# Stores of a batch's odd blocks moved from SyncE's queue to ScalarE's in a recommender kernel

## The chip, the cores and the metric

The kernel runs on one core of one Trainium2 chip. The metric is the device time of the whole program in microseconds (us). Most executions agree within 0.3%.

## The reference, cut to what matters

A table of 100001 items (rows of 128 floats) is gathered for 1024 users and 50 steps, averaged, normalized and run through a spiking neuron; the mean spike count of each user is then multiplied with the whole table.

```python
e = emb[seq]                                   # 1024 x 50 x 128
uF = jnp.cumsum(e, axis=1) / denom[:, :, None]
y = (uF - mean) * lax.rsqrt(var + BN_EPS) * gamma + beta
_, spikes = lax.scan(step, v0, x_seq)          # 50 steps
uF_out = spikes.mean(axis=0)                   # 1024 x 128
scores = uF_out @ emb.T                        # 1024 x 100001, 409.6 MB
```

## The kernel before

The first stage computes the spike counts, one step after another. The second stage goes through the table in 25 chunks of 4096 items (the last is shorter). A chunk is loaded seven chunks ahead (2 MB), transposed on TensorE into PSUM and split into a rounded part by ScalarE (`hi`) and the remainder by VectorE (`lo`). For each of the eight blocks `n` of 128 users it makes a tile of 128 x 4096 scores in four pieces `q` of 1024 columns: TensorE multiplies into a PSUM tile, VectorE evicts (copies from PSUM into the output buffer) pieces 0 and 2, ScalarE pieces 1 and 3, and the tile is stored (2 MB). (The first block of the first chunk is done apart.)

```python
def store(n, c0, o):
    nc.sync.dma_start(out=out[n * P : (n + 1) * P, c0 : c0 + o.shape[1]], in_=o)
...
op = ctx.enter_context(tc.tile_pool(name="o", bufs=3, reuse_waits="tile"))
psum = ctx.enter_context(
    tc.tile_pool(name="psum", bufs=4, space=bass.MemoryType.PSUM, reuse_waits="tile")
)
...
for c, (c0, w) in enumerate(chunks):
    for n in range(NB):
        o = op.tile([P, CH], F32, tag="o", name=f"o_{c}_{n}")
        for q in range(-(-w // HALF)):
            po = psum.tile([P, HALF], F32, tag="ps", name=f"po_{c}_{n}_{q}")
            for k0 in range(0, hw, BANK):
                product(po[:, k0 : k0 + BANK], c, q, n, k0, min(BANK, hw - k0))
            if turn % 2 == 0:
                nc.vector.tensor_scalar_mul(o[:, h0 : h0 + hw], po[:, :hw], 1.0 / T)
            else:
                nc.scalar.mul(o[:, h0 : h0 + hw], po[:, :hw], 1.0 / T)
            turn += 1
            if n == NB - 1 and q < 2:
                ready(c + 1, 2 + q)      # a quarter of the next chunk: transpose, hi, lo
        store(n, c0, o[:, :w])           # cut: the first chunk's exceptions
        if n in (2, 5):
            ready(c + 1, n // 5)
    if c + AHEAD < len(chunks):
        fetch(c + AHEAD, rowp)           # the load, by nc.sync
```

Two pools: three output buffers `o` in SBUF, and four PSUM slots.

Of the kernel before, what the change touches and what calls it, by code (L numbers as in the profile page):

```python
# [20 lines left out]
P = 128  # L21
# [10 lines left out]
def rec_kernel(  # L32
# [9 lines left out]
    nc = tc.nc  # L42
# [109 lines left out]
            )  # L152

    def store(n, c0, o):
        nc.sync.dma_start(out=out[n * P : (n + 1) * P, c0 : c0 + o.shape[1]], in_=o)


    with ExitStack() as ph:
# [193 lines left out]
        o = gp.tile([P, HALF], F32, tag="e", name="o_0_0_0")  # L352
        for h, po in enumerate(pre):
            product(po, 0, 0, 0, h * BANK, BANK)
        step(halves[1])
        nc.scalar.mul(o[:, :BANK], pre[0], 1.0 / T)
        store(0, 0, o[:, :BANK])
        lower(0, 3, pt)
        nc.vector.tensor_scalar_mul(o[:, BANK:], pre[1], 1.0 / T)
        store(0, BANK, o[:, BANK:])  # L360
        spiked(countB, slice(P, BANK), vt)
        spiked(countC, halves[1], vt)
        for q in range(1, 4):
            o = (up if q == 3 else gp).tile([P, HALF], F32, tag="uF" if q == 3 else "e", name=f"o_0_0_{q}")
            po = (accp if q % 2 == 0 else vp).tile(
                [P, HALF], F32, tag="v0" if q % 2 else "pt", name=f"po_0_0_{q}"
            )
            for k0 in range(0, HALF, BANK):
                product(po[:, k0 : k0 + BANK], 0, q, 0, k0, BANK)
            for h, cs in enumerate(halves):  # L370
                if h == 0:
                    nc.scalar.mul(o[:, cs], po[:, cs], 1.0 / T)
                else:
                    nc.vector.tensor_scalar_mul(o[:, cs], po[:, cs], 1.0 / T)
            store(0, q * HALF, o)
# [13 lines left out]
    for c, (c0, w) in enumerate(chunks):  # L389
        for n in range(NB):  # L390
            if c == 0 and n == 0:
                continue
            o = op.tile([P, CH], F32, tag="o", name=f"o_{c}_{n}")
# [40 lines left out]
```

## Time and profile before

| | before |
|---|---|
| time, median of the first 3 runs | 1699.22 us |
| first store issued | 597.00 us |
| DMA share of the second stage, 597 to 1699 us | 0.99, at 405 GB/s |
| one store, one load (2.1 MB each) | about 5 us and 6.4 us of all DMA engines (estimates of the prediction) |
| issue of a store by SyncE | 0.33 us |
| output buffers, PSUM slots | 3, 4 |

The DMA share is the mean busy share of the core's 16 DMA engines: at 0.99 the data movers set the pace, and every other engine's idle time is slack. The lines are shown in the prediction.

### The profile page before, as it was taken

What the parts mean: (1) busy time and instruction counts of PE and PEld (TensorE: products, weight loads), DVE (VectorE), ACT (ScalarE), POOL (GpSimd) and SP (SyncE); (2) the same over time, 40 slices, a digit from 0 to 9 for tenths busy, and PEclk for the clock granted to TensorE, in tenths of its full rate; (3) what the DMA queues carried; (4) which work ended last, traced back from release to release, by engine and by line L of the source; (5) the groups of instructions that cost most, each with busy time, mean ns of one, the idle gap of its engine ahead of it and who ended that gap; (6) DMA issues with size and microseconds to landing.
All of it is one profiled execution on the core that took longest, in us unless ns stands there. A gap on an engine that the chain in (4) does not pass through costs nothing.

```text
span 1698.7 us, 12572 instructions
## 1 busy us (share of the span) xinstructions
PE 1055.1 (62%) x4434; PEld 808.9 (48%) x4434; DVE 1000.2 (59%) x1211; ACT 631.3 (37%) x697; POOL 379.1 (22%) x406
## 2 busy tenths in 40 slices
PE   3222323232223297887777787777777778888886
PEld 2111212122122276665566665666655556766664
DVE  5577778776768874554455454554454555555553
ACT  2122222222222354444444444444444444444442
POOL 7666666666666200000000000000000000000000
PEclk9999999999998598999999999899999899999998
DMA  9211111111111089999999999999999999999998
GB/s 342 100 45 47 46 46 48 49 46 45 47 45 47 22 351 408 424 424 409 410 402 412 401 400 399 411 413 407 407 403 407 398 404 395 424 418 418 414 414 348
DMA packets 58412, 488.15 MB, mean 287 GB/s; under 512 B 12491, under 2 KB 13292, under 8 KB 33772
## 3 DMA queue, kind: packets, MB, share of 16 engines
q1 hardware_dynamic: 45548, 461.10, 66.2%
q0 software_dynamic: 12800, 26.24, 5.3%
q8 instruction: 35, 0.57, 0.1%
q14 instruction: 29, 0.24, 0.0%
HBM read 77.69 MB, written 409.60 MB: 287 GB/s over the span
## 4 chain that ended last, share of the span: by engine, by line
DMA 42%; DVE 24%; PE 16%; another core or an unknown queue 7%; ACT 7%; issue 3%; SPq 0%; POOL 0%; ACTq 0%; DVEq 0%; POOLq 0%
DMA scores<-o 41%; PE po L146 15%; ACT o L403 5%; DVE bs L292 4%; DVE uF L291 4%; DVE v L323 4%; DVE count L261 3%; DVE s L306 3%; DVE negv L328 2%; DVE o L401 2%; ACT v L320 1%; DVE a L314 1%; DMA e<-in_L_rec_emb_table,idx 1%; DVE mv L296 1%
## 5 line engine op out<-in xcount | busy, mean ns | idle before, releaser
L401 DVE TENSOR_SCALAR o<-po 128x1024 f32<-128x1024 f32 x390 | 462.9, 1220 | 472.6 <-DMA scores<-o 355.7
L403 ACT ACTIVATE o<-po 128x1024 f32<-128x1024 f32 (+1 forms) x390 | 385.8, 1018 | 573.6 <-DMA scores<-o 359.6
L146 PE MATMUL po<-hi,countC 128*128 128x512 f32 x784 | 344.1, 439 | 154.0 <-ACT o L403 153.8
L185 POOL DMA_INDIRECT e<-in_L_rec_emb_table,idx x400 | 378.5, 946 | 188.6 <-issue 107.9
L146 PE MATMUL po<-lo,countC 128*128 128x512 f32 x784 | 329.5, 421 | 0.0
L250 PE MATMUL pre<-zT,l 128*128 128x512 f32 x100 | 77.6, 778 | 383.6 <-DVE uF L291 329.8
L146 PEld LDWEIGHTS po<-hi,countC 128*128 128x128 f32 x784 | 163.5, 209 | 214.6 <-ACT o L403 181.2
L146 PE MATMUL po<-hi,countB 128*128 128x512 f32 x588 | 234.5, 399 | 22.3 <-ACT o L403 21.8
L250 PEld LDWEIGHTS pre<-zT,l 128*128 128x128 f32 x100 | 28.8, 289 | 425.5 <-issue 310.7
L146 PE MATMUL po<-lo,countB 128*128 128x512 f32 x588 | 229.5, 391 | 0.0
L146 PEld LDWEIGHTS po<-lo,countC 128*128 128x128 f32 x784 | 162.8, 208 | 32.2
L300 ACT ACTIVATE r<-mv,eps 128x1 f32<-128x1 f32 x50 | 14.7, 294 | 392.2 <-DVE mv L296 230.2
L134 DVE TENSOR_TENSOR lo<-pt,hi 128x1024 fp32r<-128x1024 f32 x98 | 117.3, 1216 | 47.9 <-ACT hi L130 47.9
L291 DVE SCALAR_TENSOR_TENSOR uF<-rlen,pre 128x512 f32<-128x512 f32 x100 | 67.8, 678 | 128.0 <-remote 112.1
L146 PEld LDWEIGHTS po<-hi,countB 128*128 128x128 f32 x588 | 110.7, 188 | 54.9 <-ACT o L403 31.8
L101 PE MATMUL pt<-ident,rows 128*128 128x128 f32 x782 | 107.2, 281 | 44.7 <-ACT o L403 38.3
L101 PEld LDWEIGHTS pt<-ident,rows 128*128 128x128 f32 x782 | 91.0, 144 | 70.3 <-ACT o L403 55.8
L146 PEld LDWEIGHTS po<-lo,countB 128*128 128x128 f32 x588 | 110.8, 188 | 21.9
L130 ACT CAST hi<-pt 128x1024 fp32r<-128x1024 f32 x98 | 99.0, 1010 | 42.1 <-PE pt L101 41.7
L282 PE MATMUL pre<-ident,e 128*128 128x128 f32 x400 | 98.5, 418 | 10.4 <-DMA e<-in_L_rec_emb_table,idx 8.7
L282 PEld LDWEIGHTS pre<-ident,e 128*128 128x128 f32 x400 | 83.2, 220 | 24.1 <-DMA e<-in_L_rec_emb_table,idx 12.3
L146 PE MATMUL po<-hi,countA 128*128 128x512 f32 x194 | 76.9, 396 | 1.1 <-ACT o L403 1.1
(61 smaller groups left out, 680.4 us busy)
## 6 DMA issues: line engine op xcount, KB each, us to landing
scores<-o SPq DMA_DIRECT2D x190, 2048.0 KB
rows<-in_L_rec_emb_table SPq DMA_DIRECT2D x24, 2048.0 KB
scores<-o SPq DMA_DIRECT2D x8, 848.5 KB
e<-in_L_rec_emb_table,idx POOLq DMA_INDIRECT x400
scores<-o SPq DMA_DIRECT2D x2, 1024.0 KB
scores<-o SPq DMA_DIRECT2D x3, 512.0 KB
scores<-o SPq DMA_DIRECT2D x2, 256.0 KB
rows<-in_L_rec_emb_table SPq DMA_DIRECT2D x1, 512.0 KB
```

Source lines behind the costliest of these rows:

```text
L101: nc.tensor.transpose(pt[:, k0 : k0 + kw], rows[c][:kw, q * KQ + k0 // P, :], ident[:kw, :kw])
L130: nc.scalar.copy(vh, vp)
L134: nc.vector.tensor_tensor(vl, vp, vh.bitcast(F32), ALU.subtract)
L146: nc.tensor.matmul(po[:, :kw], lhsT=counts[n], rhs=part[:, k0 : k0 + kw], start=j == 0, stop=j == 1,)
L185: nc.gpsimd.indirect_dma_start(out=es[t][:, n * P : (n + 1) * P], out_offset=None, in_=table, in_offset=bass.IndirectOffsetOnAxis(ap=idx[: ...
L250: nc.tensor.matmul(pre[h], lhsT=l, rhs=zT[:, h * BANK : (h + 1) * BANK], start=t == 0, stop=False, skip_group_check=True,)
L282: nc.tensor.matmul(pre[h][:, k : k + P], lhsT=e[:, h * BANK + k : h * BANK + k + P], rhs=ident, start=False, stop=last, is_transpose=True, ...
L291: nc.vector.scalar_tensor_tensor(uF[:, cs], rlen[:, cs], 1.0 / (t + 1), pre[h], ALU.max, ALU.mult)
L292: nc.vector.bn_stats(bs[:, h, :], uF[:, cs])
L323: nc.vector.scalar_tensor_tensor(vt[:, cs], negv[:, cs], -0.5, vt[:, cs], ALU.mult, ALU.add)
L401: nc.vector.tensor_scalar_mul(o[:, h0 : h0 + hw], po[:, :hw], 1.0 / T)
L403: nc.scalar.mul(o[:, h0 : h0 + hw], po[:, :hw], 1.0 / T)
```

## The change

The intent: two hardware queues for the stores, so that the issuing work is shared and two stores can be under way at once. Blocks with an even `n` stay with SyncE, as do all loads.

```diff
     def store(n, c0, o):
-        nc.sync.dma_start(out=out[n * P : (n + 1) * P, c0 : c0 + o.shape[1]], in_=o)
+
+        engine = nc.scalar if n % 2 else nc.sync
+        engine.dma_start(out=out[n * P : (n + 1) * P, c0 : c0 + o.shape[1]], in_=o)
```

## The prediction

> **What bounds the kernel now.** I read the page first (slices, DMA queues, chain), then the waits by engine, then the windows of the second stage, then the timeline at the end of a chunk of the table. The page's 40 slices show two stages: a first of 14 slices (about 597 us) in which VectorE leads and the DMA engines do little, and a second of 26 slices with the DMA row at 8 to 9.
>
> ```profile
> DVE  5577778776768874554455454554454555555553
> DMA  9211111111111089999999999999999999999998
> GB/s 342 100 45 47 46 46 48 49 46 45 47 45 47 22 351 408 424 424 409 410 402 412 401 400 399 411 413 407 407 403 407 398 404 395 424 418 418 414 414 348
> q1 hardware_dynamic: 45548, 461.10, 66.2%
> HBM read 77.69 MB, written 409.60 MB: 287 GB/s over the span
> DMA scores<-o 41%; PE po L146 15%; ACT o L403 5%; DVE bs L292 4%; DVE uF L291 4%; DVE v L323 4%; DVE count L261 3%; DVE s L306 3%; DVE negv L328 2%; DVE o L401 2%; ACT v L320 1%; DVE a L314 1%; DMA e<-in_L_rec_emb_table,idx 1%; DVE mv L296
> ```
>
> The stores to scores are 41% of the chain, and one hardware queue carries all 461 MB. The change touches only stores, and the first one is issued at 597.00, so the first 597 us are not in play.
>
> The windows view of the second stage and of the ends of chunks (columns: busy time and count of PE, PEld, DVE, ACT, POOL; granted clock; DMA share; GB/s):
>
> ```profile
> 597.00:1699.00 1102.00, 877.22 (x3883) 688.52 (x3881) 575.17 (x492) 479.47 (x487) 0.00 (x0) 0.93 0.99 405
> ...
> 1418.00:1423.00 5.00, 3.77 (x21) 2.96 (x21) 3.26 (x3) 2.80 (x4) 0.00 (x0) 1.00 1.03 436
> 1423.40:1425.00 1.60, 1.60 (x8) 1.31 (x7) 1.17 (x2) 0.77 (x2) 0.00 (x0) 1.00 0.15 61
> 1507.00:1508.40 1.40, 1.40 (x8) 1.17 (x7) 0.96 (x2) 0.57 (x2) 0.00 (x0) 1.00 0.37 152
> ```
>
> Over 1102 us the mean DMA engine is busy 0.99 of the time: the stage is bound by the data movers. Only for about 1.5 us at the end of a chunk does the share fall (0.15 and 0.37 here), and no wait of an issuing sequencer on a transfer explains that. The waits:
>
> ```profile
> SPq L155 <- DVE o L401: 966.8, 198, 11.6
> ACT o L403 <- DMA scores<-o: 359.6, 128, 9.1
> DVE o L401 <- DMA scores<-o: 355.7, 129, 7.9
> ```
>
> SyncE's queue waits for the evictions (the data to be stored), hardly for anything else, and the evictions wait for an output buffer to be emptied by a store. That circle says: three output buffers, emptied at the pace of the DMA engines. The issue itself is small:
>
> ```profile
> 1003.03 0.33 SPq L155 DMA_DIRECT2D scores<-o  x1
> 1003.46 0.39 SPq L79 DMA_DIRECT2D rows<-in_L_rec_emb_table  x1
> ```
>
> 0.33 us per store against about 5 us that a 2 MB store occupies the engines: SyncE issues for some 205 x 0.33 = 68 us of the 1102.
>
> **What the Trainium skill says.** "DMA: Bandwidth & Descriptors", section "Issuing engines are not separate DMA queues": DMAs from SyncE and ScalarE run on the same 16 engines and interleave, and issuing from several engines saves only the sequencer's issue time. The trace agrees with its premise: 0.33 us of issue beside 5 us of transfer. Same page, "Specifications": the fabric's ceiling is 435 GB/s; the trace has 436 in its best 5 us window and 405 over the stage, so little room is left. Same page, "Queues, rings and completion order": each DMA engine takes turns, packet by packet, between the queues that have work; with one queue for all stores, no view of before shows it for two stores. The page "Perfetto Trace Analysis", section "Identifying Performance Opportunities", says that a gap repeating on the engine that should be saturated can mean too few buffers; the dip at each chunk's end looks like one.
>
> **The change part by part.** The order view of both programs: SyncE goes from 237 to 137 instructions, ScalarE from 698 to 799; every computing instruction stays in its place, the waits of the evictions are for the same stores, and the table loads stay with SyncE. So 100 issues move.
>
> (1) SyncE loses 100 x 0.33 = 33 us of issue. It was idle for 967 us waiting for VectorE, so this is worth 0.
>
> (2) ScalarE gains 100 issues, about 100 x 0.33 = 33 us if they cost it the same, plus a wait for VectorE in front of each. In a tile of four halves VectorE evicts two (2 x 1.22, merged 2.35 us) and ScalarE two (1.94 us), started together, so ScalarE waits about 0.4 us: 100 x 0.4 = 40 us. ScalarE was busy 479 of 1102 us; with 73 more it has 550 us idle. Most of that idle time is the wait for a buffer, which lies just after the issue, so the cost on the path is near 0; only in front of the casts of the next chunk's table and of an eviction whose buffer is already free can up to 0.7 us show. One such place per chunk at its end, 24 x 0.7 = 17 us off the path, of which I count 2.
>
> (3) The bytes are the same: 409.6 MB out and, in this stage, 405 GB/s x 1102 us - 409.6 = 37 MB in. No byte is saved.
>
> (4) The loads. Load issue to load issue is 46.96 us (1003.46 to 1050.42); the chunks late in the kernel, without a load, take 40.5 us (dip at 1507.0 to dip at 1547.7). So a 2.1 MB load occupies 6.4 us, 328 GB/s, where the stores run at 16.8 MB / 40.5 = 414. If alternating with ScalarE's stores hid all of that slowness, 17 loads x (6.4 - 5.06) = 23 us would be won. I count a quarter: -5.
>
> (5) The release of buffers. With one queue a store gets all engines and buffers come free one at a time, every 5 us; when one comes free, two untouched stores (10 us of work) are still ahead of the engines. With two queues two stores share: when one ends, its companion may be almost done, and 5 to 10 us of work are left. The refill takes 2.4 us of eviction and about 1 us of issue and start (an estimate from the two timelines) where TensorE had run ahead, and 4.7 us at a chunk's end (eviction starts at 1419.72, store issued at about 1424.4), where the casts and subtractions of the next chunk lie between. So only at the chunk's end can the engines run dry longer, by perhaps 0.5 us, 24 times: 12 us; and once per load, when SyncE's stores stand behind the load while ScalarE's queue empties, by up to 1 us, 17 times. I count a third of the 29: +10, less the 3 that staggering might give back: +7.
>
> Sum: 0 + 2 + 0 - 5 + 7 = +4 us on 1699: 1703, and as I do not trust the signs of (4) and (5), I pull it towards no change: 1701.
>
> **The rivals.** Rival A: interleaving makes the transfers better, hiding the slowness of loads and the dips. For: 6.4 us for a load, dips to 0.15. At the very most it wins the 23 us of (4) and the dips, (1 - 0.15) x 1.6 = 1.4 and (1 - 0.37) x 1.4 = 0.9, about 1 us x 24 = 24: 47 us, 1652. Against: the dips come when a chunk's last tile is not evicted yet, and a second queue evicts nothing. Rival B: buffers come free in pairs, and evictions, TensorE and transfers fall into step: bursts with the engines dry in between. For: only three buffers, and slack at chunk ends is already used up. With 2 us per chunk and 2 per load: 24 x 2 + 17 x 2 = 82 us, 1780. Against: in mid-chunk the refill of 3.4 us fits into the 5 us that are left at worst. Rival C: ScalarE's in-order stream becomes the bound, as its issue waits for VectorE. Against: 550 us of idle time; it would take over 5 us per store. Rival D, which I believe: work is conserved, the engines stay at 0.99, and nothing happens beyond a few us.
>
> **Range and chances.** D with the terms above gives 1685 to 1715; part of A would go to 1680, part of B to 1725. Range 1682 to 1724. Faster by over 2% needs under 1665, nearly all of A: 4%. Slower by over 2% needs over 1733, half of B: 8%. Within 2%: 88%.
>
> **What would show it.** Right: two hardware queues with about 200 MB of stores each, ScalarE's queue (L157) with 100 or so issues near 0.33 us, DMA share still 0.98 or more from 597 us on, issue-to-issue of the loads within 0.7 us of 46.9. Step (4) right: chunks with a load shorter while those without stay at 40.5. Step (5) right: the dips at chunk ends longer, or new ones after each load, and the evictions' waits for stores in fewer and longer pieces. Wrong: if DMA share falls below 0.97, buffers are the bound and B holds; if GB/s at the same share rises above 415, A holds; if ScalarE's evictions wait less for stores and VectorE's more, C holds.

## More of the kernel before

The runs came from different chips: on some of them the kernel before took about 1616 us, on others 1694 to 1700, because the first stage ends earlier there (first store at 513 us in the profile of run e4, at 597 in that of the kernel before). The stage that matters here is as long on both. Every experiment is therefore compared with runs of the kernel before on its own chip.

## The result, and the profile after

The changed kernel took 1747.9 us (median of 4 runs, 1745.9 to 1750.7) against 1699.4 us: a ratio of 1.0286, 95% interval 1.0268 to 1.0304. Ratios are the mean time of one kernel's fast runs over that of the other's of the same rounds, so not quite the ratio of the medians. The change lost 48.5 us and was outside the predicted range. The granted clock is not the reason: in the four runs the mean was 0.78, 0.92, 0.78 and 0.93, and the times do not follow it. Its low values come from the first stage.

The page of the changed kernel, its DMA rows and its two store queues:

```profile
DMA  9211111111111299999999999999999999989998
GB/s 343 91 46 46 44 47 45 49 49 44 45 48 46 93 384 398 393 389 404 385 397 395 375 392 383 397 387 381 395 392 394 373 393 375 420 363 405 421 422 340
q1 hardware_dynamic: 31004, 256.29, 37.2%
q10 hardware_dynamic: 14544, 204.81, 27.8%
```

The windows view over the second stage of the changed kernel, and over a stretch within one chunk (columns as in the prediction; the last two are DMA share and GB/s):

```profile
597.00:1744.00 1147.00, 919.62 (x3883) 710.37 (x3882) 582.23 (x493) 486.89 (x488) 0.00 (x0) 0.92 0.96 390
...
1056.00:1061.00 5.00, 3.27 (x14) 2.07 (x13) 2.45 (x2) 1.64 (x2) 0.00 (x0) 1.00 0.76 321
1061.00:1064.00 3.00, 3.00 (x19) 2.58 (x18) 0.00 (x0) 2.04 (x2) 0.00 (x0) 1.00 0.66 268
```

The same 461.10 MB pass (256.29 + 204.81) in a stage that is 45 us longer. The DMA share fell from 0.99 to 0.96, which is 0.03 x 1147 = 34 us of idle data movers, and the dips are no longer only at the ends of chunks. (Most of the rest is in the packets: the packed traces hold the time of each, which no view prints. Summed over these queues and divided by 16 engines it grew from 1125.2 to 1134.7 us.)

Who keeps them waiting? The view of waits, before and after (columns: total us, times, longest):

```profile
ACT o L403 <- DMA scores<-o: 359.6, 128, 9.1
...
ACT o L403 <- PE po L146: 213.0, 145, 3.1
```

```profile
ACT o L405 <- PE po L146: 434.4, 302, 5.8
...
DVE o L403 <- DMA scores<-o: 211.0, 52, 6.6
...
ACT o L405 <- DMA scores<-o: 180.3, 45, 7.0
...
PE po L146 <- DVE o L403: 142.7, 115, 3.9
```

Before, the evictions mostly waited for a store to free a buffer. After, ScalarE's evictions wait twice as long for TensorE (434 instead of 213 us), and half as long for stores (180 instead of 360). The buffers had become free, but the products were not there. Yet TensorE has no more work than before. The timeline of one odd tile (block 5) in the changed kernel shows why:

```profile
1056.50 1.23 DVE L403 TENSOR_SCALAR o<-po 128x1024 f32<-128x1024 f32 x1 [0.61 <-PE po L146]
...
1057.40 1.03 ACT L405 ACTIVATE o<-po 128x1024 f32<-128x1024 f32 x1 [0.79 <-PE po L146]
1057.78 0.50 PE L146 MATMUL po<-hi,countC 128*128 128x512 f32 x1 [0.41 <-DVE o L403]
...
1059.03 1.22 DVE L403 TENSOR_SCALAR o<-po 128x1024 f32<-128x1024 f32 x1 [1.30 <-PE po L146]
1060.31 0.50 PE L146 MATMUL po<-hi,countC 128*128 128x512 f32 x1 [1.32 <-DVE o L403]
...
1061.53 1.02 ACT L405 ACTIVATE o<-po 128x1024 f32<-128x1024 f32 x1 [3.11 <-PE po L146]
...
1062.59 0.34 ACTq L157 DMA_DIRECT2D scores<-o  x1
```

Read it as a chain: the eviction of piece 0 starts at 1056.50 and ends at 1057.73; only then, at 1057.78, does TensorE begin piece 2. The eviction of piece 2 ends at 1060.25; only then, at 1060.31, does TensorE begin piece 3. From the first eviction to the issue of the store it takes 6.1 us. In the kernel before, block 5 of one chunk took 2.4 us, as all four pieces were ready:

```profile
1409.55 1.94 ACT L403 ACTIVATE o<-po 128x1024 f32<-128x1024 f32 x2 [2.65 <-PE po L146]
1409.57 2.35 DVE L401 TENSOR_SCALAR o<-po 128x1024 f32<-128x1024 f32 x2 [2.70 <-PE po L146]
...
1411.99 0.33 SPq L155 DMA_DIRECT2D scores<-o  x1
```

TensorE waits for a PSUM slot. The built programs say which slot each PSUM tile has; here chunk 10, blocks 0 to 2 and 5, in both (slots 0 to 3, pieces 0 to 3 of each block):

```
           block 0    block 1    block 2    block 5
before     1 2 3 0    2 1 0 3    1 2 3 0    1 0 3 2
changed    3 0 1 2    3 1 3 3    0 2 1 0    2 0 2 2
```

In the changed kernel, pieces 0, 2 and 3 of blocks 1 and 5 have one and the same slot. Count over the second stage after how many PSUM tiles a slot is used again (distance 1: by the very next tile). Before, the distance is 2 in 23 cases and otherwise 3 to 5; in the changed kernel it is 1 in 47 cases and 2 in 73. So a change of the issuing engine of some stores made the pool give out PSUM differently. How the pool decides was not examined; that it goes by its own estimate of when each engine will have let a slot go, and that ScalarE's new issues moved that estimate, is only argued.

The theories, then. Theory 1: the slots make the tiles late. Theory 2: two queues share the engines, and buffers come free in pairs. Theory 3: ScalarE's in-order stream is held up by issuing. Theory 4: packets that alternate between two queues are dearer in themselves.

### The profile page after: what moved, and what is told of

The parts are those of the page before. It is cut to its first block, busy times and chain, and to the rows that moved or that the text cites. A ratio compares the mean times of both kernels' runs of the same rounds, so it can differ in the third digit from the quotient of the medians.

```text
span 1744.8 us, 12375 instructions
## 1 busy us (share of the span) xinstructions
PE 1097.0 (63%) x4434; PEld 831.3 (48%) x4434; DVE 1006.9 (58%) x1211; ACT 638.6 (37%) x697; POOL 379.0 (22%) x406
## 3 DMA queue, kind: packets, MB, share of 16 engines
q1 hardware_dynamic: 31004, 256.29, 37.2%
q10 hardware_dynamic: 14544, 204.81, 27.8%
## 4 chain that ended last, share of the span: by engine, by line
PE 31%; DVE 26%; DMA 26%; another core or an unknown queue 7%; ACT 6%; issue 3%; POOL 0%; DVEq 0%; ACTq 0%
PE po L146 27%; DMA scores<-o 25%; DVE o L403 4%; ACT o L405 4%; DVE bs L294 4%; PE pt L101 4%; DVE uF L293 3%; DVE v L325 3%; DVE count L263 3%; DVE s L308 3%; DVE negv L330 2%; ACT v L322 1%; DVE a L316 1%; DMA e<-in_L_rec_emb_table,idx 1%
## 5 line engine op out<-in xcount | busy, mean ns | idle before, releaser
L403 DVE TENSOR_SCALAR o<-po 128x1024 f32<-128x1024 f32 x390 | 468.1, 1221 | 368.4 <-DMA scores<-o 211.0
L405 ACT ACTIVATE o<-po 128x1024 f32<-128x1024 f32 (+1 forms) x390 | 396.0, 1020 | 615.8 <-PE po L146 434.4
L146 PE MATMUL po<-hi,countC 128*128 128x512 f32 x784 | 350.3, 447 | 129.9 <-ACT o L405 75.5
L146 PE MATMUL po<-hi,countB 128*128 128x512 f32 x588 | 249.4, 424 | 90.2 <-DVE o L403 89.5
L146 PE MATMUL po<-lo,countB 128*128 128x512 f32 x588 | 238.7, 406 | 0.0
L146 PEld LDWEIGHTS po<-hi,countB 128*128 128x128 f32 x588 | 116.7, 198 | 141.9 <-DVE o L403 117.6
L146 PEld LDWEIGHTS po<-lo,countB 128*128 128x128 f32 x588 | 116.7, 198 | 21.8
L101 PE MATMUL pt<-ident,rows 128*128 128x128 f32 x782 | 119.9, 304 | 6.6 <-DVE rows L98 6.2
L101 PEld LDWEIGHTS pt<-ident,rows 128*128 128x128 f32 x782 | 108.0, 159 | 23.6 <-DVE rows L98 6.7
```

The source lines that it names most:

```text
L101: nc.tensor.transpose(pt[:, k0 : k0 + kw], rows[c][:kw, q * KQ + k0 // P, :], ident[:kw, :kw])
L146: nc.tensor.matmul(po[:, :kw], lhsT=counts[n], rhs=part[:, k0 : k0 + kw], start=j == 0, stop=j == 1,)
```

## The experiments

All give the correct result. Differences in us are between medians (before: 1615.95 us for the first four, 1699.75 for e5 to e8, 1616.75 for e9 to e12, 1693.92 for the last four).

| run | queues for stores | PSUM slots | change | ratio to before, 95% interval |
|---|---|---|---|---|
| e1 | two | as before | +14.2 us | 1.0085 (1.0068 to 1.0102) |
| e2 | one | as changed | +43.4 us | 1.0274 (1.0244 to 1.0305) |
| e3 | two | in turn | +16.6 us | 1.0099 (1.0082 to 1.0116) |
| e4 | one | in turn | -3.8 us | 0.9981 (0.9964 to 0.9997) |
| e5, the change again | two | as changed | +46.7 us | 1.0262 (1.0244 to 1.0281) |
| e6 | one, ScalarE's | in turn | -4.2 us | 0.9969 (0.9952 to 0.9985) |
| e7, halves | two | in turn | +10.1 us | 1.0063 (1.0046 to 1.0080) |
| e8, halves | one | in turn | +8.6 us | 1.0047 (1.0030 to 1.0063) |
| e9, 4 buffers | two | in turn | +2.0 us | 1.0012 (0.9995 to 1.0029) |
| e10, 4 buffers | one | in turn | -10.0 us | 0.9941 (0.9924 to 0.9957) |
| e11, loads on ScalarE | one | in turn | -23.8 us | 0.9855 (0.9839 to 0.9871) |
| e12, slot used twice | one | in turn but one | +1.2 us | 1.0011 (0.9994 to 1.0028) |
| e13, slot used three times | one | three in one | +34.2 us | 1.0196 (1.0179 to 1.0213) |
| e14, 4 buffers | one | as changed | +5.9 us | 1.0026 (1.0006 to 1.0046) |
| e15, loads on ScalarE | one | the pool's | -21.4 us | 0.9871 (0.9855 to 0.9888) |
| e16, loads on ScalarE, 4 buffers | one | in turn | -17.8 us | 0.9892 (0.9875 to 0.9908) |

### Slots and queues taken apart: e1 to e4

Four PSUM pools of one slot each replace one pool of four, so the kernel itself names the slot. `SLOTS` is a list of 874 digits read out of the built kernel before (e1) or the changed kernel (e2); in e3 and e4 the digit is `len(used) % 4`.

```diff
-        tc.tile_pool(name="psum", bufs=4, space=bass.MemoryType.PSUM, reuse_waits="tile")
+        tc.tile_pool(name="psum", bufs=1, space=bass.MemoryType.PSUM, reuse_waits="tile")
+    used = []
+
+    def place():
+        s = SLOTS[len(used)]           # e3, e4: str(len(used) % 4)
+        used.append(s)
+        return "ps" + s
-                po = psum.tile([P, HALF], F32, tag="ps", name=f"po_{c}_{n}_{q}")
+                po = psum.tile([P, HALF], F32, tag=place(), name=f"po_{c}_{n}_{q}")
```

(The tiles for the transposes likewise.) For e1, expected:

> The changed kernel with its two queues, but each PSUM tile put by hand into the slot that it had in the kernel before. Theory 1 (the pool gave the changed kernel another order of PSUM slots, some of them reused by the very next tile, so that TensorE cannot run ahead and the tiles of the store are filled late): back to 1695 to 1710 us. Theory 2 (two queues share the DMA engines, three output buffers come free in pairs, the engines run dry): stays at 1740 to 1755. Theory 3 (ScalarE's stream is held up by its 100 issues): stays at 1740 to 1755.

For e2:

> The kernel before with its one queue, but each PSUM tile put by hand into the slot that it has in the changed kernel. Theory 1: slow without any second queue, 1730 to 1755 us. Theories 2 and 3: 1695 to 1705, as before.

For e3:

> Two queues, PSUM slots strictly in turn (each reused after exactly four tiles). Theory 1: 1690 to 1705. Theories 2 and 3: 1740 to 1755.

For e4:

> One queue, PSUM slots strictly in turn: the control for the run with two queues and slots in turn. All theories: 1690 to 1702, as the stage is bound by the DMA engines; if slots in turn shorten the dips at the ends of chunks, up to 10 us under the kernel before.

The numbers in us of these texts were meant for a chip on which the kernel before takes 1699; on this one it took 1616, so the ratios decide. With one queue and the slots of the change (e2), nearly all of the loss is there: 43.4 us. With two queues and the old slots (e1), 14.2 us are left. Theory 1 holds for the larger part, and something of the two queues remains. The waits of e2 (first) bear the signature of the changed kernel, those of e4 (second) that of the kernel before:

```profile
ACT o L421 <- PE po L158: 441.5, 292, 5.8
...
ACT o L421 <- DMA scores<-o: 177.3, 56, 6.5
DVE o L419 <- DMA scores<-o: 163.8, 59, 5.2
```

```profile
DVE o L407 <- DMA scores<-o: 426.3, 185, 6.9
ACT o L409 <- DMA scores<-o: 388.4, 150, 8.1
...
ACT o L409 <- PE po L146: 162.7, 123, 3.2
```

e2 has the 434 us of the changed kernel (441.5) without any second queue, and its data movers are idle as often (0.96; the line of e4, at 1.00, stands with e9 and e10):

```profile
560.00:1560.00 1000.00, 813.26 (x3364) 628.39 (x3363) 503.35 (x420) 422.71 (x421) 0.00 (x0) 0.89 0.96 391
```

The page "Perfetto Trace Analysis" of the Trainium skill, section "Optimizing Tensor Performance", says that independent groups of matmuls should rotate through PSUM banks so that the eviction of one overlaps the matmuls of the next; e2 against e4 is what it costs here not to: 2.9%.

### The change on another chip: e5

No edit: it is the changed kernel.

> The changed kernel as it is, to have it on the chip of the other experiments, where the kernel before took 1616 us. 2.5 to 3.5% slower than before, as on the first chip. If the two causes add up (slots +2.7%, second queue +0.9%), 3.6%; if the second is hidden behind the first, 2.8%.

46.7 us, so the loss repeats, and it is less than 43.4 + 14.2 = 57.6: the two causes overlap in part. The sum is across chips, so I take no more from it than that.

### ScalarE's issuing: e6

On top of e4, every store and every later load is issued by ScalarE.

```diff
-        nc.sync.dma_start(out=out[n * P : (n + 1) * P, c0 : c0 + o.shape[1]], in_=o)
+        nc.scalar.dma_start(out=out[n * P : (n + 1) * P, c0 : c0 + o.shape[1]], in_=o)
     def fetch(c, pool):
+        engine = nc.scalar if c >= AHEAD else nc.sync      # and engine.dma_start below
```

> PSUM slots in turn, one queue, but it is ScalarE's: all 205 stores and the later loads are issued by ScalarE. It tells apart what is left of the slowdown once the slots are right (1.2%: 1632 against 1612 us). Theory 3 (ScalarE's in-order stream is held up by issuing): at least as slow as two queues, 1.2 to 2.5% above one queue of SyncE, as there are twice as many issues. Theory 2 (two queues share the engines, so buffers come free in pairs): within 0.5% of the kernel before.

0.3% below the kernel before, much as e4 (0.2%). Twice the issues cost nothing: Theory 3 falls.

### Sharing for one tile: e7 and e8

On top of e4, each store is cut into two halves of its columns; the halves go to both queues (e7) or both to SyncE's (e8).

```diff
     def store(n, c0, o):
-        nc.sync.dma_start(out=out[n * P : (n + 1) * P, c0 : c0 + o.shape[1]], in_=o)
+        w = o.shape[1]
+        cuts = [(0, w)] if w <= HALF else [(0, w // 2), (w // 2, w)]
+        for (a, b), engine in zip(cuts, (nc.sync, nc.scalar)):
+            engine.dma_start(out=out[n * P : (n + 1) * P, c0 + a : c0 + b], in_=o[:, a:b])
```

For e7, expected:

> PSUM slots in turn, every store cut into two halves of its columns, one half to each queue: the two queues share the engines, but they share them for one tile, so output buffers again come free one by one. Theory 2: within 0.5% of the same cut with both halves in one queue. Theory 3: 1.2 to 2.5% slower than that, as ScalarE issues 199 halves. Theory 4 (packets of two queues alternating are dearer by themselves): about 1% slower.

For e8:

> The control for the cut: both halves in SyncE's queue, PSUM slots in turn. A packet of 8 KB took 309 to 315 ns where one of 16 KB took 611 to 625, so up to 1% above the kernel before; all theories agree.

The cut itself costs 0.6 to 0.8% (8.6 us above before, e4 being 3.8 below). Two queues instead of one cost 1.5 us more, within the intervals. The packets together took as long (1141.5 us of 16 engines in e7, 1142.0 in e8). So it is not dear that two queues alternate within one tile: in this form Theory 4 falls. It leaves open whether it is dear when the two queues hold different tiles, as in e3, and whether by Theory 2 or 4.

### A fourth output buffer: e9 and e10

On top of e3 and e4. The room comes from one table buffer less, so e9, e10, e14 and e16 each change two things; no run takes them apart.

```diff
-AHEAD = 7
+AHEAD = 6
-    op = ctx.enter_context(tc.tile_pool(name="o", bufs=3, reuse_waits="tile"))
+    op = ctx.enter_context(tc.tile_pool(name="o", bufs=4, reuse_waits="tile"))
```

For e9, expected:

> PSUM slots in turn, two queues, a fourth output buffer (paid for with one table buffer less, so loads run six chunks ahead instead of seven). Theory 2 (what is left of the slowdown is buffers coming free late and in pairs): the left 1.2% goes, within 0.5% of one queue with four buffers. If it stays 1% above that, the left-over is not the buffers.

For e10:

> The control: PSUM slots in turn, one queue, four output buffers. If the dips at chunk ends (0.5 to 1 us of all 16 engines, about 20 times) are for want of a buffer, 0.5 to 1% below one queue with three, that is 0.7 to 1.3% below the kernel before; if the slowest DMA engine sets the pace, no change.

The two queues' cost shrinks from 16.6 + 3.8 = 20.4 us to 2.0 + 10.0 = 12.0 us. So 8 us go with the fourth buffer, and the expectation of Theory 2 (within 0.5%) was missed by 0.2%. With one queue the fourth buffer won 0.4%, less than the 0.5 to 1% expected. The windows from 560 to 1560 us of e3, e4, e9 and e10, in this order:

```profile
560.00:1560.00 1000.00, 806.19 (x3446) 639.20 (x3444) 513.82 (x430) 431.15 (x430) 0.00 (x0) 0.90 0.97 399
```

```profile
560.00:1560.00 1000.00, 802.74 (x3560) 623.82 (x3560) 526.25 (x445) 442.98 (x446) 0.00 (x0) 0.94 1.00 412
```

```profile
560.00:1560.00 1000.00, 790.48 (x3533) 625.43 (x3532) 524.51 (x441) 442.56 (x442) 0.00 (x0) 0.89 1.00 411
```

```profile
560.00:1560.00 1000.00, 811.25 (x3577) 630.03 (x3576) 528.55 (x449) 444.83 (x449) 0.00 (x0) 0.94 1.00 417
```

With three buffers two queues let the engines run dry (0.97 against 1.00). With four they do not, and still move 411 instead of 417 GB/s at the same share. The packet times of the traces (summed, by 16 engines) split the cost: 1128.0 us in e3 against 1123.6 in e4, and 1122.2 in e9 against 1114.0 in e10. So with three buffers some 4 of the 20 us are longer packets, the rest mostly idle engines; with four, 8 of the 12 are longer packets (those of 4 KB, of the loads, 183 ns on average instead of 174). These are single profiles; two of the changed kernel (it and e5) differ by 2.3 us. Why packets are longer stays open, and Theory 4 is not excluded for whole tiles.

The same times show that buffers do not come free in pairs. Of the 189 spaces between the ends of full stores only 2 are under 2.5 us in e3 (none in e4). What changed is how long a store takes from its first packet to its last: 6.8 us in the median instead of 5.5. So Theory 2 holds only as "buffers come free later".

### Only the loads on the second queue: e11 and e15

The second queue is given to the other direction: later loads by ScalarE, all stores by SyncE. e11 is on top of e4 (slots in turn); e15 is the kernel before with nothing else changed.

```diff
     def fetch(c, pool):
+        engine = nc.scalar if c >= AHEAD else nc.sync      # and engine.dma_start below
```

For e11, expected:

> PSUM slots in turn, all stores in SyncE's queue, only the later table loads in ScalarE's. It tells whether the left-over comes from stores sharing with stores or from the load sharing with a store. If from stores with stores: within 0.4% of the kernel before. If from the load: 0.5 to 1.2% above it.

For e15:

> The kernel before with nothing changed but that the later table loads are issued by ScalarE; the pool gives out the PSUM slots itself, and in the build it reuses none at distance one. 1 to 1.6% below the kernel before, as with slots in turn (1.4%). If the slots in turn were what gained: under 0.5%.

I had thought that e11 could only lose less; it won 23.8 us and beats both kernels, and e15 won 21.4 us by this one edit. The windows line of e11:

```profile
560.00:1560.00 1000.00, 812.39 (x3617) 628.51 (x3618) 536.42 (x456) 450.72 (x454) 0.00 (x0) 0.97 1.00 419
```

The engines are as busy as in e4, but move 419 instead of 412 GB/s. The timelines of e4 and of e11 give the time from load to load, that is per chunk (first and eleventh load of a stretch):

```profile
824.39 0.39 SPq L79 DMA_DIRECT2D rows<-in_L_rec_emb_table  x1
...
1288.12 0.39 SPq L79 DMA_DIRECT2D rows<-in_L_rec_emb_table  x1
```

```profile
818.12 0.38 ACTq L80 DMA_DIRECT2D rows<-in_L_rec_emb_table  x1
...
1271.05 0.37 ACTq L80 DMA_DIRECT2D rows<-in_L_rec_emb_table  x1
```

(1288.12 - 824.39) / 10 = 46.37 us in e4, (1271.05 - 818.12) / 10 = 45.29 us in e11: 1.08 us per chunk, times 17 chunks 18 us of the 20 between them. My first reading, that the load's slowness is hidden behind the packets of a store, is not what the packet times show. By 16 engines, the loads' packets took 144.4 us in e4 and 142.3 in e11, the stores' packets of 16 KB 952.2 and 939.7. In e4 a store's packet took 677 ns on average while a load was under way in the same queue, and 622 otherwise; in e11, with the load in the other queue, 614 and 619. So 12.5 of the 20 us are shorter packets of the stores, about half of it from those beside a load (55 ns x 1773 packets / 16 = 6 us). Why a shared queue slows them is not shown. The page "Perfetto Trace Analysis", section "DMA Optimizations", advises that inputs and outputs on separate issuing engines may make sense; here it does.

### Which feature of the slots: e12 and e13

On top of e4, in blocks 1 and 5 only: in e12 piece 3 takes the slot that piece 2 has just used; in e13 pieces 0, 2 and 3 have one slot, as in the changed kernel.

```diff
-    def place():
-        s = str(len(used) % 4)
+    def place(move=0):
+        s = str((len(used) + move) % 4)
-    ... tag=place(), name=f"po_{c}_{n}_{q}"
+    ... tag=place((1, -1, -1, -2)[q] if n in (1, 5) else 0), name=f"po_{c}_{n}_{q}"     # e13
```

For e12, expected:

> One queue, PSUM slots in turn but for one thing: in tiles 1 and 5 of each chunk the fourth half takes the slot that the third has just used (48 times in all; the changed kernel has 47 reuses at distance one). Theory 1 in its plainest form, that a reuse at distance one makes TensorE wait for an eviction of 1.22 us each time: at most 48 x 1.4 = 67 us, of which what the output buffers do not hide shows. If these alone carry the effect: 1.5 to 2.7% above the kernel before; if it takes the whole pattern (reuse at distance one and two in a row within a tile): under 0.7%.

For e13:

> One queue, PSUM slots in turn but that in tiles 1 and 5 of each chunk the first, third and fourth half all use one slot, as they do in the changed kernel. If the chain inside a tile carries the effect of the slots: 1.5 to 3% above the kernel before, where the single reuse gave 0.1%. If not, under 0.7%, and the pattern over several tiles must do it.

48 single reuses cost 1.2 + 3.8 = 5 us against e4. The chain of three pieces in one slot, 48 times, lost 34.2 us, most of what the full pattern of the change did, with the same wait:

```profile
ACT o L409 <- PE po L146: 462.1, 301, 5.8
```

One wait of TensorE per tile is mostly absorbed; two in a row (piece 2 waits for piece 0's eviction, piece 3 for piece 2's) put off the store of that tile by more than the other two buffers can cover.

### The slots with more buffers: e14; and the best of both: e16

e14 is e2 with the edit of e9; e16 is e11 with that edit. For e14, expected:

> One queue, the changed kernel's PSUM slots, a fourth output buffer. If the slots cost time because tiles are filled too late for three buffers, one buffer more takes most of the 2.7% away: under 1.2% above the kernel before. If TensorE's halts by themselves make the stage longer (production below the pace of the stores): still 2 to 2.7%.

For e16:

> Slots in turn, loads alone in ScalarE's queue, all stores in SyncE's, four output buffers: the candidate that should beat both kernels. If the gains add up (1.4% and 0.4%): 1.8% below the kernel before. If the loads' own queue has taken away the same idle time as the fourth buffer: 1.4 to 1.6%.

A fourth buffer takes the slots' cost from 2.7 to 0.3% over the kernel before (against one queue with good slots and equal buffers, from 2.9 to 0.9%). So they cost time mostly by filling tiles too late, not by overloading TensorE; the last 0.9% is not explained. In e16 the fourth buffer added nothing to the loads' own queue (1.1% won, e11 1.4%), less than either expectation; why, and whether the missing table buffer matters, was not pursued. e11 is the fastest version, e15 the simplest.

## Why the prediction was wrong

The bound was right: the data movers set the pace, at a share of 0.99. So were parts (1) to (3): SyncE's saved issues are worth nothing, ScalarE's issue takes 0.34 us and costs nothing on the path (e6), and the bytes are the same. (Two small slips hardly touch the sum: the page of the changed kernel has 101 moved issues, not 100, and the two dips named in part (4) are 40.7 us apart, not 40.5.)

The step that failed is the sentence before them: "every computing instruction stays in its place, the waits of the evictions are for the same stores". It is true and not enough. I looked at the waits of VectorE and ScalarE, but not at those of TensorE, whose instructions stand in the same order and wait for other evictions. The view of the order with its waits, available before any run, shows it: the fourth piece of block 5 waited for VectorE in both builds, but in the changed one for the eviction just before it (piece 2 of block 5 itself), in the kernel before for that of piece 2 of block 4. In the sum, the slip sits in part (5) and in the case against rival B: the refill of a buffer was taken as 2.4 us of eviction "where TensorE had run ahead"; in the changed kernel block 5 took 6.1 us, for the products were not there. From that slip the sum lacked its largest term, about 43 us (e2).

Part (5), the late release of buffers, had the right sign, and its signature (fewer and longer waits for stores) shows where the slots are equal: VectorE has 67 waits of 4.4 us on average in e3 (the line below) for 185 of 2.3 in e4. In the changed kernel (52 instead of 129) it proves nothing, as e2 with one queue has 59. Its size was off: +7 us predicted, 20.4 measured between e3 and e4, of which 8 go with a fourth buffer and 12 do not; 8 of these are longer packets, a term that the sum did not have.

```profile
DVE o L409 <- DMA scores<-o: 292.3, 67, 7.7
```

Part (4) put the gain in the wrong place. Beside stores in both queues nothing was won from the loads (47.8 us from load to load in e3, 46.4 in e4); with the loads alone in the second queue 20 us were (e11 against e4). That this is close to the 23 us that I had called the most is partly luck: the loads' own packets gave 2 of them, the stores' 12.5.

Of the rivals, D (nothing happens) fell, and C has not its sign (VectorE's waits for stores fell too, from 356 to 211 us). The observed share of 0.96 was my stated sign for B, and it would have misled: the share fell mostly because tiles were late for want of PSUM slots, and only to a smaller part because of the queues.

## What to carry to other kernels

An edit that moves no computing instruction can still change which slot of a pool each tile gets; compare the waits of every engine in both builds, and the distance at which slots are reused, before reasoning about queues. Where the data movers are the bound, a second queue for the same stream cost about 1% here (e1, e3), while a second queue for the stream in the other direction gained 1.3%. If a pool's choice hurts, name the slots by hand (one tag per slot, in turn).

## What the Trainium skill lacked or had wrong

- "DMA: Bandwidth & Descriptors", section "Issuing engines are not separate DMA queues", says that issuing from several engines saves only the sequencer's issue time. The queue mattered beyond that, both ways: loads alone in ScalarE's queue took 1.3% off the time (e15), stores split by tiles over two queues with good slots added 1.0% (e3), where all issues on ScalarE changed nothing (e6, 0.3% below the kernel before, as e4's 0.2%).
- No page has it that a change of a DMA's issuing engine can change the PSUM slots that a pool gives out: 47 reuses at distance one where there were none, worth 2.7% (e2).
- No page has how many output buffers a store stream needs when two tiles are stored at once: with three, the DMA share was 0.97 (e3), with four (and one table buffer less) 1.00 (e9).
- No page has it that a store's packets are slower while a load stands in the same queue: 677 ns instead of 622 for 16 KB (e4), and 614 with the load in the other queue (e11).
